# Weighting expert rows at their source, gathering them with an add, and adding a bias by DMA

## The chip, the cores and the metric

The kernel runs on one core of one Trainium2 chip, as one program. The metric is the device time of an execution in microseconds (us). Besides the times of whole runs there is one profiled execution, from which every duration below is taken. A core has five engines that run their own instruction streams and meet at semaphores: TensorE (PE in the profile, with PEld for its weight loads), VectorE (DVE), ScalarE (ACT), GpSimd (POOL) and SyncE (SP), which here only issues DMA transfers. POOL and ACT issue transfers too.

## The reference

Two transformer layers on 8 x 256 tokens of 512 channels, all in float32. Each layer normalizes its input and adds an attention part and a feed-forward part, which both read the normalized input, to it.

```python
def _L0_ffn_ref(xt, ...):
    ...
    gate = zeros((T, E)).at[arange(T)[:, None], idx].add(vals)   # two of 16 experts a token
    def step(y, p):
        w1, b1, w2, b2, w3, b3, ge = p
        h = silu(xt @ w1 + b1) * (xt @ w2 + b2)
        return (y + ge[:, None] * (h @ w3 + b3), None)
    y, _ = scan(step, zeros_like(xt), (ew1, eb1, ew2, eb2, ew3, eb3, gate.T))
    z = silu(xt @ sw1 + sb1) * (xt @ sw2 + sb2) @ sw3 + sb3
    return y + z

def _L1_attn_ref(x, Wqkv, bqkv, Wo, bo):
    ...
    return einsum('bqd,dc->bqc', out, Wo) + bo

def _L1_ffn_ref(x, A, B, Wr):
    ...
    h = einsum('nd,krd->nkr', xf, A)                             # 64 adapters of rank 16
    out = einsum('nkr,kdr->nd', h * G[:, :, None], B)            # G: 16 of 64, softmax
    return out * SCALING

xn = _layernorm(x)
x = x + _L0_attn_ref(xn, ...) + _L0_ffn_ref(xn, ...)
xn = _layernorm(x)
x = x + _L1_attn_ref(xn, ...) + _L1_ffn_ref(xn, ...)
```

What the change touches is the expert sum `ge * (h @ w3 + b3)` of layer one and the bias `bo` of layer two's attention.

## The kernel before

The 2048 tokens are four chunks of 512 (`NCH = 4`); a chunk is four tiles (`TPC`) of 128 rows, one row a partition. Large matrix products are done with seven block products instead of eight (p1 to p7); sums of blocks and of products are made by VectorE, ACT and POOL.

**Layer one.** After normalizing, routing and the shared expert, the loop over `plan` (from L1640) runs the attention: two passes of two chunks, eight groups of heads, two halves, seven outer products (class `Outer`), each of seven inner products. After each inner product, `slot` (L1034) runs small pieces of other work that `later` has given a due slot; a list of names in `slot` tells which pieces don't count against the limit of a slot.

Experts are done for sorted rows. `dispatch` gives each token two slots (`slots`) and two gates (`slot_gates`). `scatter` (L1484) writes each token's number into `table` at its slots, 32 times, and `read_table` reads it back into `whose`: which token a slot holds. In the second pass `expert` (L1461) makes one of 36 tiles of 128 slots: class `Expert` gathers the token rows (L1051) and the expert's weights; `turn` transposes; `bias` (L1071) gathers the rows of `b3` over the token rows; `up` makes the hidden values; `down` makes `h @ w3`, VectorE adds the `b3` rows (L1100), and the result goes to `yd` in HBM. Their due slots are 10, 11, 14 and 22 after the start. The rows in `yd` are not yet weighted.

**From layer one to layer two.** Chunk i's x tile gets a token's two expert rows by `gather` (L748: for n = 0 and 1, four indirect DMAs each, issued by POOL, into tiles of their own) and `settle` (L758: x + gate * row, VectorE, four steps for each n). For chunk 0 this is done near the end of layer one (`settled_in`, L1556, called by `wrapped_up`). For chunks 1 to 3 it is done in the loop of layer two, during the chunk before. Chunks 2 and 3 also get their attention sums there, by `finish` (L783), after `combine` (POOL) has put them together.

**Layer two** (from L1738) is a loop over the four chunks. For chunk i: the first half of the feed-forward part is `low_rank(0)` and `low_rank(2)`, each seven products (L1806) with weights `WA` and a gate applied; results are in `hg`. In `low_rank(0)` four of these gate multiplications are POOL's, one for each quarter (0,0), (1,1), (0,1), (1,0), in this order; in `low_rank(2)` VectorE does them. Then the second half with `hg` (L1913). The products run in the order p1, p2, p6, p7, p5, p3, p4 (`seven`, L1692); after each, `filled(k)` runs pieces that are written out by hand in `fill1` and `fill2`: for example `fill2[7]` runs after p7 of `low_rank(2)`. Pieces of the same chunk are the attention (`turned`, `weighed`, `attended`); pieces for the next chunk are the gathers, settling, the statistics and scaling of its normalization (`stats`, L273; `scaled`, L280). The banks are `a` (p1, p6, p5, p3), `b` (p2) and `e` (p7, p4). ACT copies a bank (L1702) into one of four `cp` buffers, which are used in turn.

`attended(t)` adds `bo` to the x tile on POOL (L1857), multiplies by `wo` (L1859) and adds that on VectorE.

In layer two VectorE, ACT and POOL run their instructions in the written order (`manual_schedule`); the order of TensorE and SP is a planner's. `WA` is loaded by `load_fa` (L927) in pieces of 512 columns: three pieces each by `load_part` 0 to 2 (L937), into token tiles whose rows have room for 3.5 such pieces, near the end of layer one, and the last five (p5's second piece, p3, p4) by SP at the start of layer two, after `wo` and `bo`.

Of the kernel before, what the change touches and what calls it, by code (L numbers as in the profile page):

```python
# [11 lines left out]
SAME = 16  # L12
# [61 lines left out]
def block_kernel(  # L74
# [567 lines left out]
    whose = [const.tile([P, n], I32, name=f"whose{n}") for n in (READ, NMT - READ)]  # L642

# [104 lines left out]
    def gather(i, n, y, ts=range(TPC)):  # L748

        for t in ts:  # L750
            at = i * TPC + t
            nc.gpsimd.indirect_dma_start(
                out=y[:, t, :], out_offset=None, in_=yd[:, :],
                in_offset=bass.IndirectOffsetOnAxis(ap=slots[:, n, at : at + 1], axis=0),
                bounds_check=NSLOT - 1, oob_is_err=False,
            )

    def settle(i, n, x_, y, ts=range(TPC)):  # L758

        for t in ts:  # L760
            gate = slot_gates[:, n, i * TPC + t : i * TPC + t + 1]
            tc.keep_in_program_order(
                nc.vector.scalar_tensor_tensor(  # L763
                    x_[:, t, :], y[:, t, :], gate, x_[:, t, :], ALU.mult, ALU.add
                )
            )
# [160 lines left out]
    def load_fa(t, lo, hi):  # L927

        for n in range(lo, hi):
# [5 lines left out]
            WA[p].append(t[:, n - lo])  # L935

    def load_part(n):  # L937

        t = toks.tile([P, 7, S], FP, tag="X", name="fa")
        load_fa(t.rearrange("p b n -> p (b n)")[:, 0 : 3 * C].rearrange("p (c k) -> p c k", c=3), 3 * n, 3 * n + 3)  # L940
# [4 lines left out]
    with in_order, tc.tile_pool(name="attn", bufs=1) as attn:  # L945
# [88 lines left out]
        def slot():  # L1034
# [3 lines left out]
            while pieces and pieces[0][0] <= now[0] and n < (2 if len(pieces) > 12 else 1):  # L1038
                f = pieces.pop(0)[2]
                f()  # L1040
                n += getattr(f, "func", f).__name__ not in ("add_a", "bias_sum", "silu", "bias", "gate", "fill_tile", "read_table", "take_table", "scatter", "load_sum", "sums1", "sums2", "sums3", "sums4", "settle0", "settle1", "out_sum", "load_sums", "store_sum", "combine", "finish", "store", "ranks", "tiles_of", "starts", "owners", "owned", "rows", "slots_of", "end", "placed", "chosen_at", "gated_at")


        class Expert:
# [31 lines left out]

            def up(self):
# [15 lines left out]
            def down(self):  # L1093
# [6 lines left out]
                add(ye, py, self.xe)  # L1100
# [360 lines left out]
        def expert(j):  # L1461
# [3 lines left out]
            later(14, e.up)  # L1465
            later(22, e.down)
# [7 lines left out]
        def beyond():  # L1474

            with tc.If(n_used[0] > USUAL):  # L1476
                for j in range(USUAL, NMT):
                    e = Expert(j)
                    e.turn()
                    e.bias()  # L1480
                    e.up()
                    e.down()

        def scatter(t, n):  # L1484

            token = small.tile([P, SAME], I32, tag="token", name="token")
            nc.gpsimd.iota(token, pattern=[[0, SAME]], base=t * P, channel_multiplier=1)
            nc.gpsimd.indirect_dma_start(
# [5 lines left out]
        def read_table(n=0):  # L1494
# [10 lines left out]
            def take_table():  # L1505
                tc.keep_in_program_order(
                    nc.vector.tensor_copy(
                        whose[n], rows.bitcast(I32).rearrange("p (j o) -> p j o", o=SAME)[:, :, 0]
                    )
                )  # L1510
# [45 lines left out]
        def settled_in(i, x_, y):  # L1556

            tc.keep_in_program_order(nc.sync.dma_start(out=x_, in_=xs_[i]))
            gathered(i, 0, y, 0)
            later(19, partial(settle, i, 0, x_, y))  # L1560
            gathered(i, 1, y, 20)
            later(39, partial(settle, i, 1, x_, y))

        def wrapped_up():

            x_, y = spare8(), spare8()
            settled_in(0, x_, y)
# [173 lines left out]
    nc.sync.dma_start(out=wo_t, in_=wo)  # L1741
    nc.sync.dma_start(out=bo_t, in_=bo.to_broadcast([P, C]))
# [15 lines left out]
    rest = work.tile([P, 5, C], FP, tag="fa", name="fa", bufs=1)  # L1758
    load_fa(rest, 9, 14)
# [18 lines left out]
    for i in range(NCH):  # L1778
# [15 lines left out]
        def low_rank(j, fill):  # L1794
# [8 lines left out]
            def product(bank, w, xx, first):  # L1803
                for n in range(2):
                    for c in range(HC):
                        mm(  # L1806
                            bank[:, bass.ts(n, S)], w[c][:, bass.ts(j + n, P)], xx[:, c, :],
# [48 lines left out]
        def attended(t):  # L1856
            add(xc[:, t, :], xc[:, t, :], bo_t, nc.gpsimd)  # L1857
# [3 lines left out]

        following = []
        if i + 1 < NCH:
            following = [next_x(i + 1), spare(), spare()]
            for n in range(TOP):
                gather(i + 1, n, following[1 + n])
        fill1 = {
            1: [partial(turned, 0)],
# [4 lines left out]
        if following:  # L1873
# [8 lines left out]

            if i:
                for k, ns in ((2, (0, 1)), (7, (2, 3))):
# [145 lines left out]
```

## Time and profile before

| | |
|---|---|
| runs: median, lowest, highest of 3 | 2644.53, 2644.34, 2647.04 us |
| profiled execution: its time, its span | 2642.12, 2640.4 us |
| granted TensorE clock, mean over the span | 0.999 |
| second layer: begins, chunk by chunk | about 2352, 2434, 2508, 2580 us |
| settling steps (L763) | 32, mostly 0.735 to 1.45 us each, longest 4.385 |
| gathers from `yd` (L752) | 32, 0.994 to 1.745 us of POOL each |
| POOL's additions of `bo` | 16, 1.259 to 1.733 us each |
| b3 gathers (L1071) | 36, 0.995 to 1.177 us of POOL each |
| VectorE's addition of b3 (`ye`) | 36, 0.679 to 0.693 us each |

How to read the profile: a row of the timeline has its start (us from the span's start), its length, the engine, the source line, the operation, `output<-inputs` by the program's names, the shapes, and how many instructions are merged in it (x8); in brackets stands the idle time ahead of it and what ended that. The span on an engine can be a sum of several instructions. A line such as L103 is a helper's (`tt`) and is told apart by its names. TensorE runs each float32 product as two passes, so that a product of four matmuls stands as x8. `POOL DMA_INDIRECT` is the time in which POOL issues a gather, not the transfer itself.

### The profile page before, as it was taken

What the parts mean: (1) busy time and instruction counts of PE and PEld (TensorE: products, weight loads), DVE (VectorE), ACT (ScalarE), POOL (GpSimd) and SP (SyncE); (2) the same over time, 40 slices, a digit from 0 to 9 for tenths busy, and PEclk for the clock granted to TensorE, in tenths of its full rate; (3) what the DMA queues carried; (4) which work ended last, traced back from release to release, by engine and by line L of the source; (5) the groups of instructions that cost most, each with busy time, mean ns of one, the idle gap of its engine ahead of it and who ended that gap; (6) DMA issues with size and microseconds to landing.
All of it is one profiled execution on the core that took longest, in us unless ns stands there. A gap on an engine that the chain in (4) does not pass through costs nothing. (4 is left out here: it accounts for less than half of the span.)

```text
span 2640.4 us, 38395 instructions
## 1 busy us (share of the span) xinstructions
PE 2612.6 (99%) x14250; PEld 2288.8 (87%) x14250; DVE 1755.3 (66%) x3211; ACT 704.3 (27%) x995; POOL 1322.1 (50%) x1297
## 2 busy tenths in 40 slices
PE   9999999999999999999999999999999999999999
PEld 6588888888888898989889898988989898977777
DVE  6795768686867686757456565656566565756774
ACT  5123232323232323232323122222312232321111
POOL 6756575656565656554534334352433453344411
PEclk9999999999999999999999999999999999999999
DMA  8996868686878777777777676777767686634201
GB/s 318 340 346 248 303 243 306 242 309 241 308 256 295 261 287 259 285 272 273 266 252 272 233 290 210 283 250 265 262 244 273 238 313 227 220 120 148 79 33 60
DMA packets 163117, 655.60 MB, mean 248 GB/s; under 512 B 19776, under 2 KB 22336, under 8 KB 160960
## 3 DMA queue, kind: packets, MB, share of 16 engines
q1 hardware_dynamic: 125504, 496.02, 53.0%
q10 hardware_dynamic: 21456, 95.95, 9.2%
q0 software_dynamic: 15968, 61.13, 6.9%
q8 instruction: 116, 1.90, 0.3%
q14 instruction: 73, 0.60, 0.1%
HBM read 512.13 MB, written 143.78 MB: 248 GB/s over the span
## 5 line engine op out<-in xcount | busy, mean ns | idle before, releaser
L1025 PE MATMUL ps_a<-xt,w 128*128 128x256 f32 x2688 | 712.6, 380 | 4.8 <-DVE c L103 4.7
L1025 PEld LDWEIGHTS ps_a<-xt,w 128*128 128x128 f32 x2688 | 470.1, 191 | 59.8 <-issue 9.3
L103 POOL TENSOR_TENSOR c<-c,r 128x512 f32<-128x512 f32 x256 | 323.2, 1286 | 247.3 <-DVE r L103 245.5
L1222 PE MATMUL ps_sc<-wo,gT 128*128 128x256 f32 x1792 | 422.4, 379 | 0.5 <-PEq L1476 0.5
L1222 PEld LDWEIGHTS ps_sc<-wo,gT 128*128 128x128 f32 x1792 | 334.3, 190 | 45.0 <-issue 2.3
L1025 PE MATMUL ps_e<-xt,w 128*128 128x256 f32 x1344 | 365.4, 381 | 3.7 <-PE ps_a L1025 3.0
L103 POOL TENSOR_TENSOR w<-w 128x512 f32<-128x512 f32 (+1 forms) x243 | 244.5, 1017 | 234.1 <-DVE w L103 194.8
L103 POOL TENSOR_TENSOR sums<-sums,sq 128x256 f32<-128x256 f32 x240 | 179.0, 746 | 313.9 <-ACT sq L1160 303.8
L1025 PEld LDWEIGHTS ps_a<-w,xt 128*128 128x128 f32 x1792 | 270.5, 191 | 23.0
L1025 PE MATMUL ps_a<-w,xt 128*128 128x128 f32 x1792 | 272.2, 274 | 0.0
L1025 PEld LDWEIGHTS ps_e<-xt,w 128*128 128x128 f32 x1344 | 230.2, 191 | 28.1 <-PE ps_a L1025 5.2
L103 DVE TENSOR_TENSOR acc<-ps_sc,acc 128x512 f32<-128x512 f32 x196 | 135.0, 689 | 153.0 <-PE ps_sc L1222 152.5
L1362 ACT COPY cp<-ps_a 128x512 f32<-128x512 f32 x160 | 93.5, 585 | 533.6 <-PE ps_a L1025 515.0
L103 DVE TENSOR_TENSOR cp<-ps_a,c 128x512 f32<-128x512 f32 x288 | 198.0, 687 | 54.1 <-PE ps_a L1025 45.7
L1169 DVE SCALAR_TENSOR_TENSOR gT<-ps_o,nw,c 128x256 f32<-128x256 f32 x256 | 112.1, 479 | 165.8 <-ACT sq L1160 139.0
L1160 ACT ACTIVATE sq<-ps_o 128x512 f32<-128x512 f32 x128 | 76.5, 597 | 485.0 <-PE ps_o L1150 445.7
L103 DVE TENSOR_TENSOR c<-ps_a,c 128x512 f32<-128x512 f32 x224 | 150.8, 684 | 76.8 <-PE ps_a L1025 75.8
L103 DVE TENSOR_TENSOR w<-w 128x256 f32<-128x256 f32 x333 | 179.1, 538 | 18.3 <-POOL w L103 14.5
L1025 PE MATMUL ps_b<-xt,w 128*128 128x256 f32 x672 | 181.9, 380 | 0.0
L103 DVE TENSOR_TENSOR s<-ps_sc,decay 128x384 f32<-128x384 f32 x256 | 141.3, 554 | 59.6 <-PE ps_sc L1137 58.1
L103 POOL TENSOR_TENSOR gT<-gT 128x512 f32<-128x512 f32 x128 | 164.8, 1288 | 5.8 <-DVE gT L1169 3.2
L1149 PE MATMUL ps_o<-s,c 128*128 128x256 f32 x512 | 154.4, 383 | 0.5
(304 smaller groups left out, 4130.1 us busy)
## 6 DMA issues: line engine op xcount, KB each, us to landing
xt<-xc SPq DMA_DIRECT2D x224, 896.0 KB
w<-in_w_att_dram SPq DMA_DIRECT2D x144, 512.0 KB
w<-in_w_att_dram SPq DMA_DIRECT2D x48, 384.0 KB
wo<-in_w_out_dram SPq DMA_DIRECT2D x56, 256.0 KB
decay<-dec SPq DMA_DIRECT2D x32, 384.0 KB
yd<-ye SPq DMA_DIRECT2D x36, 256.0 KB
wos<-wo ACTq DMA_DIRECT2D x32, 256.0 KB
wo<-wos SPq DMA_DIRECT2D x32, 256.0 KB
```

Source lines behind the costliest of these rows:

```text
L103: (eng or nc.vector).tensor_tensor(o, a, b, op)
L1025: mm(o, a, b, start=(first and ty == 0), stop=True, skip_group_check=True)
L1149: mm(po[:, bass.ts(hh, S)], v[:, 0:P], s[:, 0:S], start=True, stop=False)
L1160: nc.scalar.activation(sq, po, AF.Square)
L1169: nc.vector.scalar_tensor_tensor(gT[:, h, :], po[:, bass.ts(h, S)], nw[:, n : n + 1], self.c[:, 2 * h + t, 0:S], ALU.mult, ALU.mult,)
L1222: mm(py[:, bass.ts(t, S)], self.O[l, p][:, hh, bass.ts(t, P)], self.wo[p][:, hh, :], start=(t == 0 and hh == 0), stop=(hh == 1), skip_grou ...
L1362: nc.scalar.copy(c, bank)
```

## The change

Each slot's gate is carried in the table beside the token's number: `scatter` copies it into column 1 of its row (POOL), and `read_table` takes it out into `gate_of`. `Expert.weigh`, due 20 slots after the start, multiplies the `b3` rows by the gate on ACT; `down` multiplies the product by the gate in the same VectorE instruction that adds these rows. So `yd` holds weighted rows. `settle` is gone: a gather adds into the x tile (`compute_op=ALU.add`), first n = 0 and then n = 1 into the same rows, and has no bounds check. In layer two the gathers of the next chunk stand in `fill1[1]` and `fill1[5]`, and `finish` has moved from `fill1[2]` and `fill1[7]` to `fill2[2]` and `fill2[7]`.

POOL's additions of `bo` are replaced by four DMAs a chunk that add the row to the x tile (`biased`, in `fill1[1]`, ahead of the gathers). The load of `bo` into its tile is still issued.

`WA`'s entries become lists of blocks of 128 columns. The second piece of p5 is loaded in two halves behind the three pieces of `load_part` 0 and 1. The last loads are four pieces in place of five, and the loads of `wo` and `bo` come after them.

```diff
@@ def gather(i, n, y, ts=range(TPC)):
                 in_offset=bass.IndirectOffsetOnAxis(ap=slots[:, n, at : at + 1], axis=0),
-                bounds_check=NSLOT - 1, oob_is_err=False,
-            )
-
-    def settle(i, n, x_, y, ts=range(TPC)):
-
-        for t in ts:
-            gate = slot_gates[:, n, i * TPC + t : i * TPC + t + 1]
-            tc.keep_in_program_order(
-                nc.vector.scalar_tensor_tensor(
-                    x_[:, t, :], y[:, t, :], gate, x_[:, t, :], ALU.mult, ALU.add
-                )
+                compute_op=ALU.add,
             )
@@ def load_fa(t, lo, hi):
-            WA[p].append(t[:, n - lo])
+            WA[p].append([t[:, n - lo, bass.ts(m, P)] for m in range(4)])
+
+    split = []
@@ def load_part(n):
-        t = toks.tile([P, 7, S], FP, tag="X", name="fa")
-        load_fa(t.rearrange("p b n -> p (b n)")[:, 0 : 3 * C].rearrange("p (c k) -> p c k", c=3), 3 * n, 3 * n + 3)
+        t = toks.tile([P, 7, S], FP, tag="X", name="fa").rearrange("p b n -> p (b n)")
+        load_fa(t[:, 0 : 3 * C].rearrange("p (c k) -> p c k", c=3), 3 * n, 3 * n + 3)
+        if n < 2:
+            rest = t[:, 3 * C :]
+            nc.sync.dma_start(out=rest, in_=low[0][:, 1, C + n * S : C + (n + 1) * S])
+            split.extend(rest[:, bass.ts(m, P)] for m in range(2))
+        else:
+            WA["p5"].append(split)
@@ class Expert:
+            def weigh(self):
+
+                j = self.j
+                self.gate = gate_of[j // READ][:, j % READ : j % READ + 1]
+                nc.scalar.activation(self.xe, self.xe, AF.Copy, scale=self.gate)
...
-                add(ye, py, self.xe)
+                nc.vector.scalar_tensor_tensor(ye, py, self.gate, self.xe, ALU.mult, ALU.add)
@@ def expert(j):
             later(14, e.up)
+            later(20, e.weigh)
             later(22, e.down)
@@ def scatter(t, n):
             nc.gpsimd.iota(token, pattern=[[0, SAME]], base=t * P, channel_multiplier=1)
+            nc.gpsimd.tensor_copy(token[:, 1:2].bitcast(FP), slot_gates[:, n, t : t + 1])
@@ def take_table():
-                tc.keep_in_program_order(
-                    nc.vector.tensor_copy(
-                        whose[n], rows.bitcast(I32).rearrange("p (j o) -> p j o", o=SAME)[:, :, 0]
-                    )
-                )
+                at = rows.rearrange("p (j o) -> p j o", o=SAME)
+                for o, i in ((whose[n].bitcast(FP), 0), (gate_of[n], 1)):
+                    tc.keep_in_program_order(nc.vector.tensor_copy(o, at[:, :, i]))
@@ def settled_in(i, x_):
-            gathered(i, 0, y, 0)
-            later(19, partial(settle, i, 0, x_, y))
-            gathered(i, 1, y, 20)
-            later(39, partial(settle, i, 1, x_, y))
+            for n in range(TOP):
+                gathered(i, n, x_, 10 + 12 * n)
@@ layer two
-    nc.sync.dma_start(out=wo_t, in_=wo)
-    nc.sync.dma_start(out=bo_t, in_=bo.to_broadcast([P, C]))
...
-    rest = work.tile([P, 5, C], FP, tag="fa", name="fa", bufs=1)
-    load_fa(rest, 9, 14)
+    rest = work.tile([P, 4, C], FP, tag="fa", name="fa", bufs=1)
+    load_fa(rest, 10, 14)
+    nc.sync.dma_start(out=wo_t, in_=wo)
+    nc.sync.dma_start(out=bo_t, in_=bo.to_broadcast([P, C]))
...
         def attended(t):
-            add(xc[:, t, :], xc[:, t, :], bo_t, nc.gpsimd)
             py = ps_y()
...
+        def biased():
+            for t in range(TPC):
+                nc.gpsimd.dma_start(out=xc[:, t, :], in_=bo.to_broadcast([P, C]), accum_op=ALU.add)
+
         following = []
         if i + 1 < NCH:
-            following = [next_x(i + 1), spare(), spare()]
-            for n in range(TOP):
-                gather(i + 1, n, following[1 + n])
+            following = [next_x(i + 1)]
         fill1 = {
-            1: [partial(turned, 0)],
+            1: [partial(turned, 0), biased],
...
+            for k, n in ((1, 0), (5, 1)):
+                fill1[k].append(partial(gather, i + 1, n, following[0]))
             if i:
-                for k, ns in ((2, (0, 1)), (7, (2, 3))):
-                    fill1[k].append(lambda ns=ns: finish(i + 1, following[0], ns, tc.keep_in_program_order))
-            for n, fill, k, ts in (
-                (0, fill1, 3, (0, 1)), (0, fill1, 4, (2, 3)), (1, fill2, 2, (0, 1)), (1, fill2, 7, (2, 3)),
-            ):
-                fill[k].append(partial(settle, i + 1, n, following[0], following[1 + n], ts))
+                for ns, k in (((0, 1), 2), ((2, 3), 7)):
+                    fill2[k].append(lambda ns=ns: finish(i + 1, following[0], ns, tc.keep_in_program_order))
```

More of the change, by code (lines that the diff above doesn't have):

```diff
@@ L642, in block_kernel @@
     whose = [const.tile([P, n], I32, name=f"whose{n}") for n in (READ, NMT - READ)]
+    gate_of = [const.tile([P, n], FP, name=f"gate_of{n}") for n in (READ, NMT - READ)]
     places = const.tile([P, TOP, NTT], I32, name="places")
@@ L1040, in slot @@
                 f()
-                n += getattr(f, "func", f).__name__ not in ("add_a", "bias_sum", "silu", "bias", "gate", "fill_tile", "read_table", "take_table", "scatter", "load_sum", "sums1", "sums2", "sums3", "sums4", "settle0", "settle1", "out_sum", "load_sums", "store_sum", "combine", "finish", "store", "ranks", "tiles_of", "starts", "owners", "owned", "rows", "slots_of", "end", "placed", "chosen_at", "gated_at")
+                n += getattr(f, "func", f).__name__ not in ("add_a", "bias_sum", "silu", "bias", "gate", "fill_tile", "read_table", "take_table", "scatter", "load_sum", "sums1", "sums2", "sums3", "sums4", "settle0", "settle1", "out_sum", "load_sums", "store_sum", "combine", "finish", "store", "ranks", "tiles_of", "starts", "owners", "owned", "rows", "slots_of", "end", "weigh", "placed", "chosen_at", "gated_at")
         class Expert:
@@ L1480, in beyond @@
                     e.bias()
+                    e.weigh()
                     e.up()
@@ L1554, in gathered, with settled_in @@
                 later(after + 2 * t, partial(gather, i, n, y, (t,)))
-        def settled_in(i, x_, y):
+        def settled_in(i, x_):
             tc.keep_in_program_order(nc.sync.dma_start(out=x_, in_=xs_[i]))
-            gathered(i, 0, y, 0)
-            later(19, partial(settle, i, 0, x_, y))
-            gathered(i, 1, y, 20)
-            later(39, partial(settle, i, 1, x_, y))
+            for n in range(TOP):
+                gathered(i, n, x_, 10 + 12 * n)
         def wrapped_up():
             x_, y = spare8(), spare8()
-            settled_in(0, x_, y)
+            settled_in(0, x_)
             accs.append(x_)
@@ L1806, in product @@
                         mm(
-                            bank[:, bass.ts(n, S)], w[c][:, bass.ts(j + n, P)], xx[:, c, :],
+                            bank[:, bass.ts(n, S)], w[c][j + n], xx[:, c, :],
                             start=(first and n == 0 and c == 0), stop=(c == HC - 1),
```

## The prediction

> **What bounds the kernel.** I read the page first, then busy time by stage, then TensorE's waits, then the order of work around the longest.
>
> ```profile
> span 2640.4 us, 38395 instructions
> ...
> PE 2612.6 (99%) x14250; PEld 2288.8 (87%) x14250; DVE 1755.3 (66%) x3211; ACT 704.3 (27%) x995; POOL 1322.1 (50%) x1297
> ```
>
> TensorE is busy in 99% of the span, and no edit touches a matmul. So the most that can be won is what TensorE idles or runs slowly. By stages of 60 us (PE, PEld, DVE, ACT, POOL, granted clock, DMA share, GB/s):
>
> ```profile
> 2280.00:2340.00 60.00, 59.79 (x337) 50.98 (x336) 36.49 (x91) 22.73 (x30) 28.80 (x29) 1.00 0.36 120
> 2340.00:2400.00 60.00, 54.39 (x255) 44.76 (x254) 44.06 (x79) 11.84 (x27) 37.18 (x31) 0.97 0.64 196
> 2400.00:2460.00 60.00, 59.85 (x270) 48.66 (x269) 39.89 (x94) 11.14 (x25) 19.41 (x14) 1.00 0.28 93
> 2460.00:2520.00 60.00, 58.12 (x268) 46.43 (x267) 42.41 (x107) 11.51 (x24) 19.97 (x16) 1.00 0.23 73
> ```
>
> The second layer begins in the second row: its chunk 0 (of four) idles 5.6 us, and the only clock below 1.00 is there. From 240 to 2340 us no row of layer one idles more than 0.95 us. TensorE's waits name the causes:
>
> ```profile
> PE ps_e L1806 <- DVE cp L103: 5.1, 2, 4.1
> PE ps_a L1806 <- DMA fa<-low: 1.5, 1, 1.5
> PE ps_e L1913 <- DVE hg L103: 1.3, 2, 0.7
> ```
>
> In order of time in chunk 0 (start, length, engine, line):
>
> ```profile
> 2366.47 1.56 PE L1806 MATMUL ps_a<-ts,fa 128*128 128x256 f32 x6 [1.46 <-DMA fa<-low]
> 2381.93 2.83 DVE L763 SCALAR_TENSOR_TENSOR spare<-spare,slot_gates 128x512 f32<-128x512 f32 x2
> 2385.28 2.82 DVE L763 SCALAR_TENSOR_TENSOR spare<-spare,slot_gates 128x512 f32<-128x512 f32 x2
> 2389.63 0.66 DVE L103 TENSOR_TENSOR cp<-ps_e,cp 128x512 f32<-128x512 f32 x1
> 2390.34 3.52 PE L1806 MATMUL ps_e<-t,fa 128*128 128x256 f32 x8 [4.13 <-DVE cp L103]
> ```
>
> VectorE runs in written order. Four settling steps (L763) and two pairs of statistics stand ahead of the addition that frees bank e; product p4 waits 4.13 us for it. The p4 that follows takes 3.52 us where such a group takes 1.89: the trace's clock stands at half for 3.41 us from 2390.6 us. That is another 1.7 us lost to the same wait.
>
> **The change, part by part.**
>
> *Settling steps out.* 32 steps leave VectorE, eight of them in each of chunks 0 to 2. Alone one takes 0.735 to 0.746 us; next to POOL's additions a pair takes 2.83. In chunk 0 the two pairs ahead of bank e hold 5.65 us, more than the 4.13 us wait. What is late next: bank e's addition then stands behind the additions of `attended` 0 and 1 (0.68 us each, the first at 2381.33) and one pair of statistics (1.6 us): it can begin at 2384.2, after ACT's copy of p5 (2383.3), and end at 2384.9. TensorE wants bank e at 2386.05, or about 1.5 us sooner once p5 no longer waits (below): 0 to 0.4 us are left. I take the whole wait as gone, and with it the half clock: -4.13 - 1.7.
>
> *Split p5.* Half of p5's operand moves into space left in two token tiles, loaded before layer one ends: two more SP issues (0.32 to 0.43 us a piece) next to loads issued at 2296 and 2305 us, where TensorE idles 0.2 us in the 60 before 2340. At the start of layer two SP issues four pieces of `fa` in place of five, and `wo` and `bo` (0.34 and 0.43 us) move behind them. p5's wait of 1.46 us goes. p3's pieces are next, wanted one product (1.73 us) and one weighing (0.86 us) later; they are now first in SP's queue, 0.86 us earlier than p5's was, and without two 256 KB loads ahead. `wo` is wanted at 2375, 14 us after its new issue. -1.46.
>
> *Gathers that add.* 32 gathers stay 32, now into the x tile itself. Chunk 0's first four for chunk 1 no longer need a `spare` tile, which POOL awaited until 2359.65 (13.44 us idle); the x tile was loaded by an SP issue at 2315.74. They can go out from 2346, while DMA moves 1 to 119 GB/s. The second four wait on POOL for the first four to land (the same rows) and are issued after hg of (1,1). No accumulating DMA is in this trace, so both prices are bounded.
> - Issue on POOL: a plain gather takes 0.994 to 1.745 us, plus 0.30 between. I take 1.30 as now; twice that, 2.6, is the far end.
> - Landing: by the landing events of POOL's queue, the eight gathers of 2359.65 to 2369.04 landed 6.3 to 14.7 us after issue, amid the fb loads; the eight of 2393.62 to 2404.38 in 3.1 to 4.1. At the slow rate (256 KB per 2.55 us) the second four, issued from 2368.7, land at about 2375, 2378, 2381 and 2384; statistics 0 and 1 want the first two at 2381, 2 and 3 the rest at about 2384. I take that: nothing lost. At twice the transfer time the last lands near 2393, and VectorE, which stops at the statistics, holds hg and so L1913: up to 6 us.
>
> *What queues behind them on POOL* is hg of (0,1) and (1,0), multiplied on POOL. The second copy by ACT in `low_rank(2)` writes the buffer that hg(1,0) of `low_rank(0)` frees, and p5 needs the bank that this copy empties. Chunk 1 shows the room:
>
> ```profile
> 2445.56 1.71 POOL L103 TENSOR_TENSOR hg<-cp,spread_g 128x512 f32<-128x512 f32 x1 [3.91 <-DVE cp L103]
> 2455.53 0.59 ACT L1702 COPY cp<-ps_a 128x512 f32<-128x512 f32 x1 [3.73 <-PE ps_a L1806]
> 2457.86 1.89 PE L1806 MATMUL ps_a<-ts,fa 128*128 128x256 f32 x8
> ```
>
> From 2447.3: four gathers at 1.30 (2452.5), hg 1.44 and 1.71 (2455.6), the copy 0.59: 2456.2, against 2457.86. Room 1.6 us; cost 0. At 2.6 us each the copy ends at 2461.4: 3.6 us lost.
>
> *Bias by DMA.* Four POOL additions a chunk (5.85 to 6.31 us) go; four DMA issues come. Nearest rows: a direct POOL store, 0.55 to 0.60 us, and the gather, 1.745. I take 1.0, by the gather. They stand ahead of the gathers, right after the last POOL work of the stage before, and `attended` wants them 15 us later or more: 0 on the path. If that cover went, one landing of 3 to 4 us.
>
> *Finish moved.* For chunks 2 and 3 the addition of layer one's sums moves to where the second settling stood. With POOL's seven `acc` additions beside it (10.5 us) a pair costs like a contended settling, 2.83; so chunk 1's wait of 0.99 us stays. In chunk 2 POOL is idle; its wait is nothing already.
>
> *Layer one.* 36 weighings on ACT: the nearest row, a 128x512 copy, 0.585 us, to the square's 0.597; ACT is busy 10 to 23 of 60 us there. Each waits for the b3 gather, which lands 4.0 to 9.9 us after issue, and 3.8 us or more before the down product; the weighing stands two slots (about 1.34 us each) ahead of that, so it finds its row there. What is behind it on ACT are PSUM copies (0.59 us) with one product (0.87 us) of room. Cost 0, at worst 36 x 0.1 = 3.6 us. 36 additions become scalar_tensor_tensor: 0.69 to at most 0.96 us (twice the 128x256 form's 0.479). 32 small copies on POOL: 0.14 us by the iota, at most 0.75; 16 us of POOL at most, in 700 us where POOL idles 14 to 32 of 60. Two copies of the table: 0.6 us. All of these lie beside a TensorE that is 59 to 60 of 60 busy; I take 0, bounds -0.5 and +4.
>
> *Given back.* With a faster chunk 0, the wait of L1913 for hg (0.75 and 0.51 us in chunks 1 and 2, none in chunk 0) should appear in chunk 0: +0.7.
>
> Sum: -4.13 - 1.7 - 1.46 + 0.7 = -6.6 us. The profiled execution took 2642.1 around its span of 2640.4; it becomes 2635.5. The median of the runs is 2.4 above it: 2644.5 - 6.6 = **2637.9 us**.
>
> **Rules against it.** In "DMA: Bandwidth & Descriptors", "Rules for kernel authors", the Trainium skill says that an accumulating DMA reads its destination and writes it later, so one must await the other's completion. No run here shows it; that serial order is in the steps above, so it moves no term. "SBUF — State Buffer", on the trap of DVE blocking DMA, says that a software DMA of some 620 ns took some 3100 ns beside a VectorE copy, for want of descriptors. The row differs: gathers here stay at 0.994 to 1.745 us beside a VectorE busy 40 to 44 of 60 us. By the page's ratio of five, an estimate, each would cost 5 us of POOL and the four 20, and chunk 1 would lose some 14 us; I keep the rows.
>
> **Rivals.**
> 1. *The wait moves to the gathers.* In chunk 0 they land late beside fb, and the statistics take the settling's place. For it: 14.7 us landings there. Against it: half of them leave that stretch. At the twofold transfer -6.6 + 6 gives 2643.9; half of that, 2641.
> 2. *POOL becomes the bound: slower.* Issue of an adding gather (place: between hg(1,1) and hg(0,1), chunks 0 to 2) decides from 1.7 us on (1.6 us of room over four); beyond it each chunk loses four times the excess. At 2.6 us, 3.6 x 3 = 10.8, less the 6.6: 2648.7; slower by over 0.2% from 2.7 us (4 x 1.0 x 3 = 12). For it: a gather that adds is more to describe. Against it: 29 of the 32 plain ones are within 1.3 us.
> 3. *The cover is thin in layer one*: ACT waits for b3 rows; 3.6 us of it leaves 2641.5.
> 4. *It does not bring what it says*: bank e is late for another reason (spread_g lands at 2380.1 in chunk 0) and half of the wait stays, with no half clock or with it: 2640 to 2642.
>
> **Chances.** Measurement tells 0.2% (5.3 us) from nothing. Forecast 0.56; rival 1 0.17, rivals 3 and 4 0.15 together: these are within 0.2%; rival 2 0.12, of which 0.10 over 0.2% slower and 0.02 within. So faster 0.56, same 0.34, slower 0.10. Upwards the range goes to 2645.5, over rivals 1, 3 and 4; downwards to 2633.5: all the waits listed (5.1 + 1.5 + 1.3) and the clock's 1.7 give 2634.9, less 1.4 for smaller waits (0.9 us of L1913 for cp among them) and the runs' spread. The forecast's own range is 2634 to 2639.
>
> **What would show it.** Right: clock 1.00 in all of layer two, p4 of chunk 0 with a wait under 1 us, no wait of p5 for `fa`, POOL's gathers at 1.0 us with hg(1,0) over before ACT's copy. Wrong: statistics (L273) of chunk 0 waiting for a DMA (rival 1); ACT's copy L1702 waiting for POOL (rival 2); ACT idle ahead of the weighing (rival 3). A landing of the second four gathers after 2385 us, or an issue over 1.7 us, makes the prediction wrong.

## The result, and the profile after

The changed kernel is slower: median 2661.21 us of 6 runs (2658.89 to 2664.57) beside 2645.45 of the kernel before on the same chip (6 runs, 2644.07 to 2647.87); ratio 1.006, 95% interval 1.0047 to 1.0072. That is 15.8 us more, where 6.6 less were forecast. The profiled execution took 2659.76 us.

The head of the page:

```profile
span 2657.9 us, 38382 instructions
...
PE 2617.3 (98%) x14250; PEld 2292.1 (86%) x14250; DVE 1726.2 (65%) x3181; ACT 726.1 (27%) x1031; POOL 1334.3 (50%) x1329
```

VectorE has lost 29 us of work and 30 instructions, as meant, and POOL has 12 us more. TensorE's busy time has grown by 4.7 us with the same 14250 matmuls: part of the loss is half clock. The stretches of 60 us around and in layer two (busy us of PE, PEld, DVE, ACT, POOL, then granted clock, DMA share, GB/s):

```profile
2280.00:2340.00 60.00, 55.71 (x336) 49.83 (x335) 34.60 (x71) 22.05 (x29) 37.61 (x37) 0.99 0.64 179
2340.00:2400.00 60.00, 59.20 (x262) 46.63 (x261) 33.34 (x89) 12.15 (x28) 24.66 (x19) 0.98 0.53 160
2400.00:2460.00 60.00, 58.15 (x271) 47.49 (x271) 30.14 (x86) 11.36 (x24) 21.31 (x16) 1.00 0.45 103
2460.00:2520.00 60.00, 52.30 (x229) 40.97 (x228) 36.10 (x94) 10.13 (x21) 22.13 (x17) 0.94 0.41 84
2520.00:2580.00 60.00, 55.67 (x256) 45.83 (x255) 35.42 (x90) 10.14 (x18) 15.07 (x12) 0.97 0.31 64
```

The second row, chunk 0, was the only bad one before (54.39) and is nearly full now. The first (59.79 before), the fourth (58.12) and the fifth (59.34) have become the bad ones. TensorE's waits put names to them:

```profile
PE ps_e L1810 <- DVE cp L103: 10.0, 2, 5.7
PE ps_a L1024 <- DVE c L103: 7.3, 9, 1.4
PE ps_sc L799 <- DVE head L103: 3.9, 1, 3.9
PE ps_sc L1862 <- DVE spare L103: 1.8, 1, 1.8
PE ps_sc L296 <- DVE spare L280: 1.8, 2, 1.1
```

To add stalls and half clock in one figure I took from the trace, for each matmul, the time from its start to the next one's start less the median of that distance for its form, and summed it: TensorE's *lost time*. Its growth of 17.5 us is the growth of the span:

| stretch, us | before | after | change |
|---|---|---|---|
| 0 to 180 | 8.6 | 9.6 | +1.0 |
| 180 to 2280 (layer one) | 17.7 | 20.4 | +2.7 |
| 2280 to 2340 (its tail) | 1.2 | 6.2 | +4.9 |
| 2340 to 2400 (chunk 0) | 8.5 | 2.4 | -6.1 |
| 2400 to 2460 | 0.5 | 2.5 | +2.1 |
| 2460 to 2580 (chunks 1 and 2) | 4.3 | 16.8 | +12.5 |
| 2580 to the end | 1.2 | 1.6 | +0.4 |

**Chunks 1 and 2.** Chunk 1's order of work after the change, from the timelines of POOL, SP, VectorE and TensorE (start, length, engine, line):

```profile
2450.19 1.26 POOL L103 TENSOR_TENSOR hg<-cp,spread_g 128x512 f32<-128x512 f32 x1 [3.91 <-DVE cp L103]
2451.60 1.57 POOL L753 DMA_INDIRECT x<-yd,slots  x1
2453.47 1.56 POOL L753 DMA_INDIRECT x<-yd,slots  x1 [0.30 <-issue]
...
2457.18 1.56 POOL L753 DMA_INDIRECT x<-yd,slots  x1 [0.30 <-issue]
2458.16 3.10 POOL L103 TENSOR_TENSOR hg<-cp,spread_g 128x512 f32<-128x512 f32 x2
...
2460.08 2.53 SPq L911 DMA_DIRECT2D spread_g<-gd  x4
...
2466.82 1.46 DVE L103 TENSOR_TENSOR hg<-cp,spread_g 128x512 f32<-128x512 f32 x1 [8.54 <-DMA spread_g<-gd]
2468.20 0.68 DVE L103 TENSOR_TENSOR spare<-ps_sc,spare 128x512 f32<-128x512 f32 x1
2468.80 2.82 DVE L780 SCALAR_TENSOR_TENSOR x<-acc,rms,x 128x512 f32<-128x512 f32 x2
...
2475.78 3.51 PE L1810 MATMUL ps_e<-t,fa 128*128 128x256 f32 x8 [5.73 <-DVE cp L103]
```

An adding gather holds POOL for 1.56 us and the next follows 0.30 later. Behind the four stand hg of (0,1) and of (1,0). The `spread_g` tiles have two buffers; `low_rank(2)` needs them anew, and they come free with exactly these two multiplications. So SP issues the loads at 2460.08, where it did at 2448.97 before; 4.6 of these 11.1 us were lost earlier, since hg of (1,1) itself comes at 2450.19 and not at 2445.56. VectorE waits 8.54 us, and all that is written behind on it is late: the attention's additions, layer one's sums (L780), the statistics, and the addition that frees bank e for p4. TensorE's waits of 1.83 and 5.73 us follow, and 6.83 us at half clock. Chunk 2 has the same picture:

```profile
2546.39 0.69 DVE L103 TENSOR_TENSOR hg<-cp,spread_g 128x512 f32<-128x512 f32 x1 [7.50 <-DMA spread_g<-gd]
...
2553.17 3.03 PE L1810 MATMUL ps_e<-t,fa 128*128 128x256 f32 x8 [4.31 <-DVE cp L103]
```

In the kernel before, VectorE already waited a little for the same loads, in chunk 1 (the first two lines) and in chunk 2:

```profile
2448.97 4.17 SPq L920 DMA_DIRECT2D spread_g<-gd  x4
...
2454.01 1.36 DVE L103 TENSOR_TENSOR hg<-cp,spread_g 128x512 f32<-128x512 f32 x1 [0.36 <-DMA spread_g<-gd]
...
2527.90 0.97 DVE L103 TENSOR_TENSOR hg<-cp,spread_g 128x512 f32<-128x512 f32 x1 [0.74 <-DMA spread_g<-gd]
```

**Layer one's tail.** POOL's first four gathers for chunk 1 went out at 2327, ahead of layer one's last sums (timelines of POOL, ACT, TensorE):

```profile
2327.08 1.67 POOL L753 DMA_INDIRECT spare<-yd,slots  x1 [2.58 <-PE ps_o L1155]
...
2333.78 2.12 POOL L103 TENSOR_TENSOR sums<-sums,sq 128x256 f32<-128x256 f32 x2
...
2335.93 0.60 ACT L1165 ACTIVATE sq<-ps_o 128x512 f32<-128x512 f32 x1 [8.46 <-POOL sums L103]
...
2338.11 5.37 PE L799 MATMUL ps_sc<-yT,wsm 128*128 128x512 f32 x8 [3.94 <-DVE head L103]
```

POOL's sums come late, so ACT's next square has no free `sq` tile and VectorE's gate products and routing stand behind it. Layer one's part and layer two's each keep the written order on POOL, but nothing ties the one behind the other: a gather whose x tile is loaded can be put into layer one.

### The profile page after: what moved, and what is told of

Its sections match the earlier page's. It is cut to its first block, busy times and chain, and to the rows that moved or that the text cites. A ratio compares the mean times of both kernels' runs of the same rounds, so it can differ in the third digit from the quotient of the medians.

```text
span 2657.9 us, 38382 instructions
## 1 busy us (share of the span) xinstructions
PE 2617.3 (98%) x14250; PEld 2292.1 (86%) x14250; DVE 1726.2 (65%) x3181; ACT 726.1 (27%) x1031; POOL 1334.3 (50%) x1329
## 5 line engine op out<-in xcount | busy, mean ns | idle before, releaser
L1024 PEld LDWEIGHTS ps_a<-xt,w 128*128 128x128 f32 x2688 | 470.5, 191 | 62.3 <-DVE c L103 10.2
```

The source lines that it names most:

```text
L1024: mm(o, a, b, start=(first and ty == 0), stop=True, skip_group_check=True)
```

## The experiments

Each row is a kernel of its own; ratios are to the kernel before, on the same chip. Medians of different rows come from several chips, on which the kernel before had medians of 2644.27 to 2645.56. The last three columns are lost time in us, in the profiled execution. The first 180 us are left out: there it went from 8.6 to 13.0 us among executions of kernels that are alike in that stretch.

| run | median us | ratio, 95% interval | tail, 2280 to 2340 | chunks 1 and 2, 2460 to 2580 | all after 180 |
|---|---|---|---|---|---|
| before | 2644.53 | | 1.2 | 4.3 | 33.4 |
| after | 2661.21 | 1.006 (1.0047 to 1.0072) | 6.2 | 16.8 | 49.9 |
| e1 four spread buffers | 2654.58 | 1.0035 (1.0023 to 1.0046) | 4.3 | 10.2 | 42.7 |
| e2 gathers behind hg | 2661.58 | 1.0065 (1.0048 to 1.0082) | 5.1 | 14.3 | 49.8 |
| e3 first gathers behind hg(0,0) | 2672.85 | 1.0103 (1.0085 to 1.0121) | 1.0 | 17.4 | 62.0 |
| e4 no gate copies | 2658.97 | 1.0053 (1.0037 to 1.007) | 6.6 | 16.4 | 47.0 |
| e5 second gathers early | 2648.24 | 1.0015 (1.0005 to 1.0024) | 6.2 | 2.9 | 36.3 |
| e6 first gathers tied | 2656.12 | 1.0043 (1.0026 to 1.006) | 1.0 | 18.3 | 46.7 |
| e7 plain gathers | 2650.98 | 1.002 (1.001 to 1.0029) | 3.1 | 13.7 | 40.5 |
| e8 p5's split alone | 2646.52 | 1.0006 (0.9995 to 1.0016) | 1.4 | 4.4 | 32.5 |
| e9 e5 and e6 | 2643.46 | 0.9993 (0.9985 to 1.0002) | 1.0 | 4.1 | 32.5 |
| e10 gap, wide scatter | 2638.7 | 0.9975 (0.9966 to 0.9985) | 1.2 | 2.6 | 25.9 |
| e11 and chunk 0 early | 2635.55 | 0.9969 (0.9957 to 0.998) | 1.2 | 2.2 | 24.8 |
| e12 e10 and sums first | 2633.94 | 0.9964 (0.9951 to 0.9977) | 1.2 | 0.9 | 24.7 |
| e13 two hg on VectorE | 2652.95 | 1.0026 (1.0015 to 1.0038) | 4.8 | 10.3 | 43.5 |
| e14 sums first alone | 2652.75 | 1.003 (1.0018 to 1.0042) | 5.0 | 8.8 | 40.9 |
| e15 all | 2633.78 | 0.9955 (0.9941 to 0.9968) | 1.2 | 0.9 | 22.4 |

**e1.**

```diff
-            return spread_into(work.tile([P, 2, CH], FP, tag="spread", name="spread_g"), i, j)
+            return spread_into(work.tile([P, 2, CH], FP, tag="spread", name="spread_g", bufs=4), i, j)
-        return work.tile([P, TPC, C], FP, tag="spare", name="spare")
+        return work.tile([P, TPC, C], FP, tag="spare", name="spare", bufs=1)
```

> Edit: the spread_g tiles get four buffers (the spare tile, used once a chunk now, gets one instead of two, so the space is the same); every instruction and every engine's order stay as after the change. Theory 1 (buffers: the second four gathers hold POOL, the two multiplications hg of the first half come late, and only they free the buffers that the spread_g loads of the second half wait for): the loads are issued within 2 us of where SP could first issue them, VectorE's wait for spread_g (8.5 us in chunk 1) falls under 1 us, TensorE's waits of 5.7 and 4.5 us in the second half's products p4 fall under 1 us and the half clock behind them goes: 2661 - 11 = about 2650. Rival A (VectorE is late by its own load: the sums of layer one moved beside POOL's additions): the waits of p4 stay at 3 us or more, 2658 to 2661. Rival B (my rival 2: ACT's copy waits for the buffer that POOL's late multiplication frees, or something else behind POOL): the wait moves to ACT's copy, and p5 or p4 still loses 2 us or more in chunks 1 and 2: 2654 to 2661.

6.6 us came back, not 11. In chunk 2 p4 no longer waited. In chunk 1 it still did (timelines of POOL, VectorE and TensorE):

```profile
2460.35 3.11 POOL L103 TENSOR_TENSOR hg<-cp,spread_g 128x512 f32<-128x512 f32 x2
...
2460.51 5.94 DVE L103 TENSOR_TENSOR hg<-cp,spread_g 128x512 f32<-128x512 f32 x1
...
2466.98 2.83 DVE L780 SCALAR_TENSOR_TENSOR x<-acc,rms,x 128x512 f32<-128x512 f32 x2
...
2475.39 3.78 PE L1810 MATMUL ps_e<-t,fa 128*128 128x256 f32 x8 [5.24 <-DVE cp L103]
```

The wait for the load is gone, but VectorE's multiplication, 0.69 us alone, took 5.94 beside POOL's late pair and the additions behind it, and the sums' pairs 2.83 beside those. ACT's copies waited for no POOL work: rival B falls, rival A has a part in chunk 1.

**e2.**

```diff
-            for k, n in ((1, 0), (5, 1)):
+            for k, n in ((1, 0), (4, 1)):
```

> Edit: in all of chunks 0 to 2 the second four adding gathers are issued at the end of the first half's steps, behind the two multiplications hg on POOL and not between them; spread_g keeps its two buffers. Theory 1 (POOL's place holds the buffers): spread_g is issued some 10 us earlier in chunk 1, as before the change (about 1.5 us behind the multiplication), TensorE's waits of 5.7 and 4.5 us go: about 2650. It may give some back: the gathers land 3 to 5 us later than now, and where the statistics have to wait for them (chunk 0 above all, where the first half is the busiest for DMA) up to 3 us are lost there: 2650 to 2653. Rival A (VectorE's own load): waits stay, 2658 to 2661. Rival B (anything behind POOL, ACT's copy too): goes like theory 1; this run doesn't tell B from 1, the run with four buffers does.

No gain. The loads of `spread_g` came in time (VectorE waited 0.25 us), but layer one's sums now waited 3.81 us for the gathers' landing and p4 5.77 for VectorE. Behind the multiplications is as bad a place as between them, by another wait. Chunk 0 lost 3.3 us more than after the change, about what was allowed for.

**e3.**

```diff
-            1: [partial(turned, 0), biased],
-            2: [partial(turned, 1)],
+            1: [partial(turned, 0), *([biased] if i else [])],
+            2: [partial(turned, 1), *([] if i else [biased])],
-            for k, n in ((1, 0), (5, 1)):
+            for k, n in ((1 if i else 2, 0), (5, 1)):
```

> Edit: for chunk 0 alone the four bias DMAs and the first four gathers are written one step later, behind the first multiplication hg, so that on POOL they stand behind all of layer one's sums and gate products. Theory 2 (four gathers ahead of layer one's last sums delay ACT's squares, then VectorE's gates, then the products L799): POOL's sums at 2333.8 start some 7 us sooner, ACT's wait of 8.46 us for them goes, TensorE's 3.94 us wait at 2338 and its half clock go, and with them 5 to 6.6 us: 2655. Chunk 0 may lose up to 2 us of this where the gathers land later. Rival (the delay there comes from something else, such as the two loads more on SP, or from layer one that runs late as a whole): POOL's order changes and the wait at 2338 stays above 2 us: 2659 to 2661.

The tail's stall went (1.0 us left), but chunk 0 lost 15.7 us in one wait, which neither theory had. ACT and TensorE there:

```profile
2403.09 0.59 ACT L1706 COPY cp<-ps_a 128x512 f32<-128x512 f32 x1 [18.77 <-POOL hg L103]
...
2403.73 3.78 PE L1810 MATMUL ps_a<-yT,fa 128*128 128x256 f32 x8 [15.72 <-ACT cp L1706]
```

The second four gathers waited on POOL 8.61 and 2.61 us for the first four to land, and hg behind them held the `cp` buffer. That is the path of the prediction's rival 2 (ACT's copy behind POOL), with its price when POOL is 19 us late.

**e4.** The copies are left out, so the gates that are read back are not the gates.

```diff
-            nc.gpsimd.tensor_copy(token[:, 1:2].bitcast(FP), slot_gates[:, n, t : t + 1])
```

> Edit: the 32 small POOL copies of a gate into the scattered row are left out (the gates read back are then not the gates; nothing else changes). Theory 3 (these copies lengthen each scatter on POOL, whose sums and gate products TensorE's groups wait for between 180 and 860 us): TensorE's lost time up to 2280 us falls by the 3.5 us that it grew: 2657.5. Rival (the longer expert rows: scalar_tensor_tensor on VectorE or the weighing on ACT): no change beyond 1 us, and the groups between 180 and 860 us still lose 0.3 to 0.6 us more than before. Rival (nothing of either: the difference is spread by chance over the groups): the lost time of single groups moves about, the sum stays.

Layer one's lost time fell from 20.4 to 17.6 us (17.7 before the change): the groups at 317 to 847 us lose 0.65 us again, not 0.95. The copies were the cause. One takes 0.185 us and the scatter behind it waits 0.59 us in place of 0.28: 0.5 us a scatter on POOL.

**e5.**

```diff
-            for k, n in ((1, 0), (5, 1)):
+            for k, n in ((1, 0), (1 if i else 5, 1)):
```

> Edit: in chunks 1 and 2 the second four adding gathers follow the first four at once, in the 32 us that POOL idles ahead of the first multiplication hg; chunk 0 stays as after the change. The two earlier runs showed that in chunk 2 the held spread_g buffers are the whole loss, and that in chunk 1 VectorE is also slowed beside POOL (a multiplication hg of 5.94 us, pairs of layer one's sums of 2.83). Theory 1 (POOL's place is the cause of both, by the late multiplications hg): the waits of p4 for VectorE are gone in chunk 2 and at most 2 us in chunk 1, no half clock there: 2661 - 11 = about 2650. Rival A (VectorE's own load, since the sums of layer one stand in fill2): chunk 1 still loses 3 us or more with its half clock, 2653 to 2655. Rival (the second gathers wait for the first to land and hold POOL up to the multiplication): hg late as now, 2658 or more.

13 us came back, and lost time in chunks 1 and 2 fell from 16.8 to 2.9, below the kernel before. Chunk 1 (POOL, SP, VectorE, TensorE):

```profile
2419.02 1.55 POOL L753 DMA_INDIRECT x<-yd,slots  x1 [0.30 <-issue]
...
2452.70 1.26 POOL L103 TENSOR_TENSOR hg<-cp,spread_g 128x512 f32<-128x512 f32 x1 [0.68 <-ACT cp L1821]
...
2453.99 3.90 SPq L911 DMA_DIRECT2D spread_g<-gd  x4
...
2459.12 0.69 DVE L103 TENSOR_TENSOR hg<-cp,spread_g 128x512 f32<-128x512 f32 x1 [0.28 <-DMA spread_g<-gd]
...
2468.76 1.99 PE L1810 MATMUL ps_e<-t,fa 128*128 128x256 f32 x8 [0.24 <-DVE cp L103]
```

The eighth gather was issued 26 us before the first multiplication of chunk 1 (2445.58). With that the load is in time, VectorE's multiplication is short, and the sums in their new place cost p4 only 0.24 us. So POOL's place caused both the held buffers and the slow VectorE.

**e6.** Chunk 0's bias DMAs are written behind its first gathers, and every gather of layer two is tied behind the POOL instruction written before it:

```diff
+            kept(nc.gpsimd.indirect_dma_start(
...
+                fill1[k].append(partial(gather, i + 1, n, following[0], kept=tc.keep_in_program_order))
```

> Edit: chunk 0's first four gathers and then its bias DMAs are tied behind POOL's last instruction of layer one, ahead of the first multiplication hg (the earlier run of this kind put them behind that multiplication, and the second four then delayed the next ones by 19 us). Theory 2: gathers from about 2349 to 2357 by that run's times, POOL idles there up to 2370; TensorE's 3.94 us wait at L799 and its half clock go, chunk 0 stays as after the change: 2661 - 5.5 = 2655.5. Rival (landing: the gathers now go out amid the fa loads, the second four wait for them on POOL, and hg(0,1) and ACT's copy behind it come late): chunk 0 loses 2 us or more, 2658 to 2665.

As theory 2 says: the tail lost 1.0 us and the median fell by 5.1. But the rival's path shows too: a piece of `fa` now landed late beside the gathers (a product waited 1.79 us for it), and chunk 0's stretch lost 4.9 us in place of 2.4.

**e7.** The gathers overwrite in place of adding, so the sums are left out.

```diff
-                compute_op=ALU.add,
+                bounds_check=NSLOT - 1, oob_is_err=False,
```

> Edit: the gathers overwrite instead of adding (their sums are left out, so x of chunks 0 to 3 holds the second choice's rows alone); places, count and bytes read stay. This prices the adding form. Theory (price and place both count): a gather takes 1.0 us of POOL instead of 1.56, four 5.2 instead of 7.4; in chunks 1 and 2 spread_g is issued some 2.2 us earlier, the waits of p4 fall by 2 us each, and the wait at L799 by 2: 2661 - 6 = about 2655, still slower than before the change. Rival (price alone: with the plain form the room is enough, as my prediction worked out): all three stalls go, 2645. Rival (place alone: the multiplications are late either way): within 2 us of 2661.

2650.98, ratio 1.002: 10 us less than with the adding form, yet slower than before. At 1.02 us a gather, SP issued `spread_g` at 2453.75 and VectorE waited 5.17 us for it; p4 waited 4.7 us in chunk 1 and 3.1 in chunk 2. By lost time the adding form makes 9.4 us (49.9 against 40.5), spread over several stretches: 3.1 in the tail and 3.1 in chunks 1 and 2. In chunks 1 and 2 it is the smaller part: 9.4 of the 12.5 us stay, so the place alone is too tight even at the price that I had forecast.

**e8.** The kernel before with p5's split and the later loads of `wo` and `bo`, as in the change's own diff.

> Edit: the kernel before with one part of the change alone: p5's operand split into the token tiles' spare room, and wo and bo loaded behind the rest of fa. My prediction has -1.46 us for it (the wait of p5 for fa in chunk 0). If bank e's wait of 4.13 us sits behind it in the same chunk, it takes this over: p4 would then wait longer by as much, since VectorE's settling steps set when it starts. Theory: p5's wait goes and p4's grows by 1 to 1.5 us: within 0.5 us of before. Rival: the parts add, 1.5 us faster.

In chunk 0 the trace speaks for the rival: p5's wait went (6.5 us lost, not 8.5) and p4's stayed at 4.17 us. Behind it 0.6 us came back, so that 0.9 us of lost time were won after 180 us. In the times this doesn't show: the interval holds 1, and this execution lost 3.3 us more in its first 180 us.

**e9.** e5 and e6 in one kernel.

> Edit: both moves of gathers together: in chunks 1 and 2 the second four follow the first four at once (alone: 2661 to 2648), and chunk 0's first four stand behind layer one's last POOL instruction (alone: 2661 to 2656). If theories 1 and 2 are two separate losses, they add: 2648.2 - 5 = about 2643, within 0.2% of before (2644.5). Rival (they share something, and the second finds little left): 2646 to 2648.

2643.46: the two losses add, and with both mended the changed kernel is as fast as the kernel before, no more. In chunk 1 p4 waited 1.45 us.

**e10.** e5's order; `gated` is the list of POOL's gate products in layer one, and the last but one is followed by 11 to 12 us of idle time; and the tokens of eight scatters are made at once:

```diff
+                with tc.issue_after(gated[(-2, -1)[n]].ins):
+                    gather(1, n, following[0])
...
-            nc.gpsimd.iota(token, pattern=[[0, SAME]], base=t * P, channel_multiplier=1)
-            nc.gpsimd.tensor_copy(token[:, 1:2].bitcast(FP), slot_gates[:, n, t : t + 1])
+            if t % 8 == 0:
+                nc.gpsimd.iota(tokens_, pattern=[[P, 8], [0, SAME]], base=t * P, channel_multiplier=1)
+                nc.gpsimd.tensor_copy(tokens_[:, :, 1].bitcast(FP), slot_gates[:, n, t : t + 8])
```

> Edit: second four early in chunks 1 and 2; chunk 0's first four tied behind layer one's last but one group of gate products on POOL (an idle stretch of 11 to 12 us ahead of its last sums, before the fa loads), chunk 0's bias DMAs and second four as after the change; and the tokens and gates of eight scatters made by one iota and one copy on POOL in place of eight of each. Theories 1, 2 and 3 add, and the 1.8 us that a product waited for fa beside the moved gathers goes: 2643 - 1.8 - 2 = about 2639 to 2641, 0.1 to 0.2% faster than before. Rival (the scatters cost TensorE nothing in this form or the other): 2641 to 2643, with 0.95 us lost in each group between 317 and 850 us instead of 0.65.

2638.7, within what was expected. Layer one lost 16.1 us, less than before the change.

**e11 and e12.** e11 puts chunk 0's second four gathers into `fill1[1]` too, behind layer one's last gate product. e12 takes e10 and puts `finish` back into `fill1[2]` and `fill1[7]`.

> Edit: as the run before it, and chunk 0's second four also ahead of the first multiplication hg on POOL (idle there from about 2350 to 2370). Theory: the stalls left in chunk 0 after the change (transposes that wait for VectorE behind statistics that waited for the second gathers, 0.9 + 1.3 + 0.9 us) shrink by some 2 us: 2637 to 2639. Rival (DMA: the gathers go out amid the fa loads, and p3 waits for its piece as in the earlier run): 1 to 2 us are lost there, 2639 to 2642.

> Edit: as the run with the gathers in the gap, and layer one's sums (finish) of chunks 1 and 2 back in the first half's steps, where they stood before the change. This tests the part of the change that moved them beside POOL's additions (pairs of 2.83 and 2.66 us there, 0.84 us each alone). Theory: with spread_g on time VectorE has the room, TensorE loses nothing to them: within 1 us of the run without this edit. Rival A (they load VectorE where it is short): 1 to 3 us faster.

2635.55 and 2633.94. By lost time each is worth 1.1 to 1.2 us over e10, which for e12 is rival A's outcome; the medians differ by more, but the runs' ranges overlap (e10: 2635.04 to 2640.91, e12: 2633.41 to 2636.74). e11 took chunk 0's stretch from 4.1 to 1.9 us and gave 1.6 back at chunk 1's p4, which waited 1.44 us; in e12 products of chunk 1's second half no longer wait for hg (0.69 us in e10).

**e13.**

```diff
-                    tt(o, c.rearrange("p (n s) -> p n s", n=2), gates2[h][:, :, bass.ts(b, S)], ALU.mult, nc.gpsimd)
+                    tt(o, c.rearrange("p (n s) -> p n s", n=2), gates2[h][:, :, bass.ts(b, S)], ALU.mult,
+                       nc.gpsimd if i in (0, NCH - 1) or h == b else nc.vector)
```

> Edit: the changed kernel with the two multiplications hg that stand behind the second gathers on POOL in chunks 1 and 2 given to VectorE, at the same place of its written order; the gathers stay where the change put them and spread_g keeps its two buffers. Theory 1, stated narrowly (it is these two multiplications, held on POOL, that hold the spread_g buffers): spread_g is issued within 2 us of VectorE's second one, TensorE's waits of 5.7 and 4.5 us go, and VectorE's next multiplication takes 0.7 to 1.5 us, not the 5.94 and 3.50 that it took beside POOL's pair in the run with four buffers: 2661 - 11 = about 2650. Rival (the gathers themselves disturb VectorE or the DMAs in that stretch, whoever does the multiplications): a wait of 2 us or more stays in chunk 1, 2653 to 2658.

Between the two: chunk 2 lost 0.85 us at p4, chunk 1 4.4. VectorE freed the first buffer early and SP issued at once, but the load took long:

```profile
2456.72 3.90 SPq L911 DMA_DIRECT2D spread_g<-gd  x4
...
2466.39 0.69 DVE L103 TENSOR_TENSOR hg<-cp,spread_g 128x512 f32<-128x512 f32 x1 [3.88 <-DMA spread_g<-gd]
```

9.7 us from the issue to the multiplication, and 8.5 in chunk 2, where e5, whose gathers were long done, had 5.1 and 5.3. So gathers in this place delay the loads in two ways: through the buffers, and by being in flight beside them. The second I had not expected; by what the loads are slowed there is not shown. The multiplication itself took 0.69 us, not 5.94.

**e14.** `finish` back in `fill1`, the gathers as the change has them.

> Edit: the changed kernel with layer one's sums (finish) of chunks 1 and 2 back in the first half's steps; the gathers stay. Rival A (VectorE's load behind the late spread_g, 2.82 + 1.40 us of sums in chunk 1 and 2.8 in chunk 2, decides how long p4 waits): p4's waits shrink by about these, from 5.7 to 1.5 to 2 us and from 4.5 to 1.7, spread_g stays late: 2661 - 7 = about 2654. Theory 1 alone (spread_g's landing decides, the sums are in its shadow): waits within 1 us of 5.7 and 4.5, 2660 to 2661. A third outcome (the second gathers now wait for the sums, hold POOL longer): spread_g later than now, no gain or a loss.

Rival A's numbers: VectorE still waited 7.24 us for `spread_g` in chunk 1, but p4 waited 1.66 us in chunk 1 and 1.66 in chunk 2; 2652.75. Chunk 1 (VectorE, TensorE):

```profile
2465.51 1.42 DVE L103 TENSOR_TENSOR hg<-cp,spread_g 128x512 f32<-128x512 f32 x1 [7.24 <-DMA spread_g<-gd]
...
2470.37 1.99 PE L1810 MATMUL ps_e<-t,fa 128*128 128x256 f32 x8 [1.66 <-DVE cp L103]
```

It takes both, the late load and the sums behind it, to make p4 wait 5.7.

**e15.** e11 and e12 together: the best order found. Its stretches:

> Edit: all mended places together: chunk 0's first four gathers in POOL's gap ahead of layer one's last sums, all second four behind the first four ahead of the multiplications hg, tokens and gates of eight scatters in one, layer one's sums in the first half. If chunk 0's second gathers and the sums' place are separate gains (each 1 us by TensorE's lost time): about 2632 to 2633 against 2644.5 before, ratio 0.995 to 0.996. Rival (they save the same wait): 2634 to 2636, as each alone.

```profile
2280.00:2340.00 60.00, 59.66 (x345) 51.93 (x345) 35.77 (x82) 22.74 (x30) 38.40 (x37) 1.00 0.55 157
2340.00:2400.00 60.00, 59.15 (x284) 49.00 (x284) 38.81 (x88) 13.53 (x28) 32.00 (x26) 1.00 0.71 187
2400.00:2460.00 60.00, 59.85 (x264) 47.78 (x263) 31.55 (x93) 11.66 (x25) 23.15 (x17) 1.00 0.43 106
2460.00:2520.00 60.00, 59.84 (x282) 49.29 (x281) 35.10 (x93) 11.26 (x24) 22.55 (x16) 1.00 0.47 100
```

2633.78, ratio 0.9955 (0.9941 to 0.9968): 11.8 us below the kernel before. All four rows are at 59 us or more and the clock stays full. By lost time the two edits add, and a little more (22.4 us against 24.8 and 24.7, from 25.9 in e10); by the medians e15 can't be told from e12 alone, and its median lies between what the two readings expected.

## Why the prediction was wrong

- **Settling steps out, split p5: right, but for what is given back.** Forecast for chunk 0: -4.13, -1.7 and -1.46, +0.7 given back. Measured: -6.1 in its stretch; neither p5 nor p4 waits there. Given back were 2.1 us, so that 4.0 are left of the 6.6; and not at L1913 but at the transposes (L296, 0.70 and 1.13) and L807 (0.73), behind statistics that waited 1.29 and 0.65 us for the second gathers: a small part of rival 1.
- **The step that failed: "Room 1.6 us; cost 0".** Two things were wrong in it. The issue was taken as a plain gather's, 1.30 with the gap; an adding one has 1.86. And the room was measured at one follower of POOL's hg, ACT's copy. The nearer follower was SP, whose `spread_g` loads wait for the buffers that hg frees. There the room was nothing: in the trace of before VectorE already waited 0.36 us for `spread_g` in chunk 1 and 0.74 in chunk 2, and the chain of waits held that load in both chunks. By e7 the step would have failed at 1.30 as well. It cost 12.5 us in chunks 1 and 2, of which 9.4 stay with plain gathers (e7). Rival 2 named the place and the sign, but not the path and the size. Its point of 1.7 us a gather counts the gap, as its sum does; 1.86 lies 0.16 above it, and by its rule that is 4 x 0.16 = 0.6 us a chunk, some 2 us in three. And its path went through ACT, which waited for no POOL work in layer two of the changed kernel; only e3 shows that path.
- **"They can go out from 2346" failed.** The written order holds within a layer, not across. 2346 is where layer one's last POOL work ended before; I read it as an order, but only the wait for a `spare` tile had held the gathers behind it. Without that wait they went out at 2327 and cost the tail 4.9 us; e6 gave these back.
- **"All of these lie beside a TensorE that is 59 to 60 of 60 busy; I take 0": mis-sized.** Layer one lost 2.7 us more, inside the bounds of -0.5 and +4, and by the copies on POOL, not by the weighings on ACT (rival 3).
- **Finish moved at no cost: wrong beside a late load, and not quite right without one.** With the load late the sums take 4 us of p4's 5.73 in chunk 1; with them in their old place 4.5 of the 12.5 us are left (e14). With the gathers early p4 of chunk 1 waits 0.24 us in e5, but 1.45 in e9 and 1.44 in e11, where VectorE waited 0.8 us for the load; with the sums back in their old place as well it doesn't wait (e12, e15).
- **Bias by DMA: right.** 0.87 to 1.43 us each on POOL, and no wait of `attended` for one; the additions left POOL without a trace in TensorE's waits.
- Two small readings in the prediction are off without consequence: by its own row TensorE wants bank e at 2386.21 (2390.34 less 4.13), not at 2386.05, and 20 us for four gathers would cost chunk 1 some 13 us, not 14.

## What to carry to other kernels

Before something is put between two instructions of a queue, list every buffer that the instructions behind it free, and who waits for each: the tightest room counts, and a wait of a few tenths in the profile says that it is already used up. Taking away a wait also takes away what it ordered: what was held back by it goes out as early as its data allow, into work it was never meant to meet. An operation's new form needs its own price in the place where it stands; here the same eight gathers cost 13 us or nothing, by whether they stood between two waited-for multiplications or in the idle time ahead of them.

## What the runs showed of the hardware

- A gather of 128 rows of 2 KB that adds holds POOL for 1.56 us (1.54 to 2.38, 32 of them), against 1.02 for the gather without the addition and with the bounds check (e7).
- Loads of `spread_g` took 8.5 to 9.7 us from issue to the multiplication with adding gathers in flight (e13). They took 5.1 to 5.6 where the gathers were long done (e5, e9, e11), and 5.7 to 6.7 in the changed kernel, where SP issued them behind the last gather's issue.
- A VectorE multiplication of two SBUF operands that started 0.16 us after one on POOL took 5.94 us, and 3.50 where no POOL additions followed (e1), in place of 0.69. The Trainium skill's "SBUF — State Buffer", "Who interferes with whom", says that such a VectorE instruction contends with a POOL instruction that reads SBUF, by an exclusive lock, and that issue order decides who blocks. The two cases agree in sign, but 5.94 us is longer than one of the POOL instructions beside it (about 1.6); and e5 doesn't fit, where it took 0.69 us in the middle of POOL's additions. What decides is open.
- The same page's trap of software DMAs beside VectorE, by which the prediction estimated 5 us a gather, did not show: the adding gathers stayed at 1.54 to 2.38 us beside a VectorE that was busy 30 to 40 of 60 us. The page tells it of a VectorE copy.
- The half clock is no plain function of one stall: it came after stalls of 1.66 and 2.05 us (e14, chunk 2; e2, chunk 0) and stayed away after one of 3.72 us (e14, the tail) and another of 1.66 (e14, chunk 1).
